# Layer 1 attention: float32r scores accumulated by key differences, two heads a pass, masking by zero values

## The chip, the core and the metric

One Trainium2 chip, one core. The core has five engines: TensorE (PE in the profile; its weight loads are PEld), VectorE (DVE), ScalarE (ACT), GpSimd (POOL) and SyncE (SP), which here only issues DMA transfers. Sixteen DMA engines move data between HBM and the on-chip memory SBUF. Matrix products land in PSUM, eight banks of 128 partitions by 512 fp32 values. The metric is the device time of one execution in microseconds (us), taken as the median of several runs; a profile is one further execution, recorded by the hardware.

## What is computed

Sixteen batches of x (512 rows of 256) and a context (1601 rows of 256) with an integer mask go through two layers, each an attention and a feed-forward part. Only the attention of layer 1 is changed:

```
xn = layernorm(x)
q, k, v = xn @ Wq.T + bq, ctx @ Wk.T + bk, ctx @ Wv.T + bv     # 16 heads of 16
scores  = q k^T / sqrt(16);  scores = where(mask == 0, -1e9, scores)
x = x + softmax(scores) v @ Wo.T + bo
```

Layer 0 is a local attention (a window of 64 keys) and a recurrent gate over the batches; the last part of layer 1 is a mixture of 8 experts of which each token takes 2.

## The kernel before

The kernel has three stages, one after the other. Layer 0 (to about 1366 us of the span) also prepares, late in the stage, the keys of batch 0 for layer 1. The attention of layer 1 follows (its scores run from 1440 to 4796 us), and then the experts (from 4875 us). Inside each stage the program order is written out by hand: `at(when, fn, ...)` puts a piece of work at a chunk number, the pieces are sorted by it, and every engine and the DMA queue of SP take their instructions in that order. The queue of SP is served in order: an instruction that waits holds back all that follow it.

**Loops of layer 1.** A batch has 16 heads in `NG` = 4 groups of 4, and its 1601 keys (padded to `SKP` = 1604) in `NCH` = 13 chunks of 128, the last of 65. The main loop (line 1318) counts chunks `n`; a batch takes `PER` = 52 of them, all batches 832. In each chunk it issues:

- `score` (line 1205): for each of the four heads, the transposed scores of one key chunk (128 keys by 512 queries) as an fp32 product with 32 rows of contraction, into one of four PSUM banks "e"; then four exponentials on ACT into `pt`. The 32 rows of a head are 16 of the head's components, one row that adds the mask bias, one that adds the negative row maximum, and 14 unused ones. The operands `ke` and `qe` are loaded by `load_ke` and `load_qe`.
- `value` (line 1222) for the chunk before: probabilities times values, four heads side by side in one PSUM bank "pv". Each head's values have a seventeenth column of ones, which sums the probabilities. With three pairs of maxima in a chunk it comes in two halves of 256 queries.
- `max_pair` (line 961), two or three times: row maxima for a group that comes 18 chunks later (`LEAD`). Here queries and keys are split in a high and a low half of their bits (`split`, line 154), stacked to 64 rows for a head (16 components times four combinations of high and low), and multiplied as float32r, two heads at a time, into two of three PSUM banks "m"; DVE reduces each bank.
- whatever `at` has put at this chunk: projections, normalisation, loads, stores, routing.

**Keys.** `key_pieces` (line 150) makes the keys of a batch: `project`, `mean`, `fill`, `add`; then `halve` stores them to `ke_d` and splits them, and `store` writes the halves to `ks_d`, each half twice (`r` is the place among the four combinations). All of this goes through HBM: `ks_d` is read back by `load_ks` (one transfer of 128 partitions for a pair of heads, 802 KB), `ke_d` by `load_ke` (one of 802 KB for a group).

**Maxima.** `shift_a` and `shift_b` (lines 984 and 991) reduce the maxima, turn them and store them into the row of `qe_d` that the scores read. **Mask.** `apply_masks` (line 368) makes bias rows, `mask_bias` (line 912) copies them into `ke_d`; `constant_rows` (line 334) fills the fixed rows of both tensors during layer 0.

Of the kernel before, what the change touches and what calls it, by code (L numbers as in the profile page):

```python
# [21 lines left out]
P = 128  # L22
# [36 lines left out]
def tile_kernel(ctx: ExitStack, tc: tile.TileContext, a, out):  # L59
# [73 lines left out]
    ke_d = [dram.tile([NG, P, SKP], F32, name=f"ke_d{i}") for i in range(2)]  # L133
    qe_d = [dram.tile([NG, P, S], F32, name=f"qe_d{i}") for i in range(2)]
    ks_d = [dram.tile([H // 2, P, SKP], F32, name=f"ks_d{i}") for i in range(2)]
    qs_d = [dram.tile([H // 2, P, S], F32, name=f"qs_d{i}") for i in range(2)]
    m_d = dram.tile([B, SKP], F32, name="m_d")
    mb_d = dram.tile([B, SKP], F32, name="mb_d")
# [5 lines left out]
    def stacked(t_d, m, r):  # L144
        return t_d[4 * m : 4 * m + 4].rearrange("p (h r d) n -> (p h) r d n", h=2, r=4)[:, r]

    def slotted(t_d, m):
        return t_d[2 * m : 2 * m + 2].rearrange("g (j s) n -> (g j) s n", s=32)[:, 0:HD, :]

    def key_pieces(pool, bank, bufs, pieces=2):  # L150
# [23 lines left out]
        def project(b, m, i):  # L174
# [3 lines left out]
            if i == 0:  # L178
                st[b, m, "k"] = pool.tile([P, SKP], F32, name="kc", bufs=bufs.get("kc", 2))
                st[b, m, "sum"] = pool.tile([P, 4], F32, name="ksum")  # L180
            ps = bank()
            for k in range(2):
# [8 lines left out]
                out=st[b, m, "k"][:, c0 : c0 + n],  # L191
# [17 lines left out]
        def part_of(h):  # L209
            return slice(h * KN, (h + 1) * KN)  # L210
# [8 lines left out]
        def add(b, m, h):  # L219
            k = st[b, m, "k"][:, part_of(h)]  # L220
            nc.vector.scalar_tensor_tensor(
                k, k, cols[:, BK1 + m : BK1 + m + 1], st.pop((b, m, "u")), ALU.add, ALU.add
            )

        def halve(b, m, h):
            k = st[b, m, "k"][:, part_of(h)]
            nc.sync.dma_start(out=slotted(ke_d[b % 2], m)[:, :, part_of(h)], in_=k)
            st[b, m, h, "halves"] = split(k, "k", KN)

        def store(b, m, h):  # L230
            hi, lo = st.pop((b, m, h, "halves"))
            for r, t in ((0, hi), (2, hi), (1, lo), (3, lo)):
                nc.sync.dma_start(out=stacked(ks_d[b % 2], m, r)[:, :, part_of(h)], in_=t)

# [9 lines left out]
            store=store,  # L244
        )


    with ExitStack() as l0:
# [80 lines left out]
        krow = wp.tile([P, SKP // 4], F32)  # L329
        nc.gpsimd.tensor_copy(krow, cols[:, KROW : KROW + 1].to_broadcast([P, SKP // 4]))  # L330
        qrow = wp.tile([P, S // 4], F32)
        nc.gpsimd.tensor_copy(qrow, cols[:, QROW : QROW + 1].to_broadcast([P, S // 4]))

        def constant_rows(i, g):
            for t_d, row in ((ke_d, krow), (qe_d, qrow)):
                nc.sync.dma_start(
                    out=t_d[i][g].rearrange("p (r n) -> p r n", r=4),
                    in_=row[:, None, :].to_broadcast([P, 4, row.shape[-1]]),
                )

# [3 lines left out]
        def load_masks():  # L346
            n = n4
            mask_i = wp.tile([n, SKP // 4], I32)
            nc.sync.dma_start(out=mask_i, in_=a["mask"].rearrange("b (r n) -> (b r) n", r=4))
            mask["i"] = mask_i  # L350

        def count_masks():
# [13 lines left out]
            mask.update(keep=keep, count=count, own=own, dg=dg)  # L366

        def apply_masks():
            n, keep, count, own, dg = (n4, *(mask[i] for i in ("keep", "count", "own", "dg")))
# [5 lines left out]
            nc.vector.tensor_mul(dg, own, qscale[0:n, :])  # L375
            nc.vector.tensor_reduce(count, dg, AX.X, ALU.add)
            nc.vector.tensor_single_scalar(count, count, 1.0e9 * HD**0.5, op=ALU.mult)
            nc.vector.tensor_scalar(keep, keep, 1.0, count, ALU.subtract, ALU.mult)
            nc.sync.dma_start(out=mb_d.rearrange("b (r n) -> (b r) n", r=4), in_=keep)
# [364 lines left out]
        for i in range(2 * NG):  # L744
            at(58 + 16 * i, constant_rows, i // NG, i % NG)
# [3 lines left out]
        for m in range(2):  # L749
# [5 lines left out]
            for h in range(4):  # L755
                at(o + 64 + 16 * h, keys.fill, 0, m, h)
                at(o + 69.5 + 16 * h, keys.add, 0, m, h)
                at(o + 73.5 + 16 * h, keys.halve, 0, m, h)
                at(o + 77 + 16 * h, keys.store, 0, m, h)
# [24 lines left out]
    with ExitStack() as l1:  # L784
# [23 lines left out]
        for t in vts:  # L808
            nc.gpsimd.memset(t, 0.0)
            nc.gpsimd.memset(  # L810
                t[:, :, 0 : H * VW].rearrange("p c (h d) -> p c h d", d=VW)[:, :, :, HD : HD + 1],
                1.0,
            )
# [3 lines left out]
        LEAD = 18  # L817

# [68 lines left out]
        def project_q(b, m):  # L887
# [14 lines left out]
            state[b]["qc", m] = qc, *keys.split(qc, "q", S)  # L902

        def store_q(b, m):
            qc, hi, lo = state[b].pop(("qc", m))
            nc.sync.dma_start(out=slotted(qe_d[b % 2], m), in_=qc)
            for r, t in ((0, hi), (1, hi), (2, lo), (3, lo)):
                nc.sync.dma_start(out=stacked(qs_d[b % 2], m, r), in_=t)

        keys = key_pieces(pool, bank, {})  # L910

        def mask_bias(b):
            rows_d = ke_d[b % 2].rearrange("g (j s) n -> (g j) s n", s=32)
            nc.sync.dma_start(
                out=rows_d[:, HD, :], in_=mb_d[b : b + 1, :].to_broadcast([H, SKP])
            )
# [8 lines left out]
        def project_v(b, p):  # L925
# [3 lines left out]
            for c in range(2 * p, min(2 * p + 2, NCH)):  # L929
                kn, o = kn_of(c), (c - 2 * p) * P  # L930
                for k in range(2):
# [8 lines left out]
            nc.scalar.copy(  # L940
                vts[p][0:kn, 0:n, 0 : H * VW].rearrange("p c (h d) -> p c h d", d=VW)[
                    :, :, :, 0:HD
                ],
                ps[0:kn, 0 : n * D].rearrange("p (c h d) -> p c h d", c=n, h=H),
# [5 lines left out]
        def load_ks(b, p):  # L950
            kst[b, p] = pool.tile([P, SKP], F32R, name="ks", bufs=3)
            nc.sync.dma_start(out=kst[b, p].bitcast(F32), in_=ks_d[b % 2][p])

        def load_qs(b, g):
            qst[b, g] = pool.tile([P, 2, S], F32R, name="qs")
# [35 lines left out]
        def shift_b(b, g):  # L991
# [4 lines left out]
            nc.vector.tensor_copy(nmT, ps[0:HD, 0:P])  # L996
            nc.sync.dma_start(
                out=qe_d[b % 2][g, HD + 1 : P : 32, :].rearrange("j (q p) -> j q p", p=P),
                in_=nmT,
            )  # L1000

        kts, qts = {}, {}

        def load_ke(b, g):
            kts[b, g] = pool.tile([P, SKP], F32, name="ke")
            nc.sync.dma_start(out=kts[b, g], in_=ke_d[b % 2][g])

        def load_qe(b, g):
            qts[b, g] = pool.tile([P, S], F32, name="qe")
            nc.sync.dma_start(out=qts[b, g], in_=qe_d[b % 2][g])  # L1010
# [191 lines left out]
        probs = {}  # L1202
        pvs = {}

        def score(b, g, c):
            kt, qt, kn = kts[b, g], qts[b, g], kn_of(c)
            scs = [psum.tile([P, S], F32, name="e", tag="e", bufs=4) for j in range(4)]
            for j, sc in enumerate(scs):
                r0 = 32 * j
                nc.tensor.matmul(  # L1210
                    sc[0:kn, :],
                    lhsT=kt[r0 : r0 + 32, c * P : c * P + kn],
                    rhs=qt[r0 : r0 + 32, :],
                    start=True,
                    stop=True,
                )
            for j, sc in enumerate(scs):
                pt = pool.tile([P, S], F32, name="pt", bufs=NPT)
                nc.scalar.activation(pt[0:kn, :], sc[0:kn, :], AF.Exp)  # L1219
                probs[b, g, c, j] = pt  # L1220
# [25 lines left out]
        for b in range(B):  # L1246
            s0 = b * PER
            at(s0 - 58, mask_bias, b)
            if b:
                at(s0 - 81, keys.mask_rows, b)  # L1250
            for m, os, o in (
                (0, (-75, -73, -71, -68), (-67, -67, -64, -62, -60, -63, -60, -58, -56)),
# [337 lines left out]
```

## Time and profile before

| | us |
|---|---|
| median of 3 runs | 5832.95 (5831.14 to 5835.01) |
| the profiled execution, its own time | 5856.85 |
| its span, first to last instruction | 5855.0 |
| layer 0, to the first product of the maxima | 1366.6 |
| layer 1, first to last score | 3355.9 |
| experts, first product to the end | 980 |

Over the span PE is busy for 5518.5 us (94%), DVE for 3405.4 (58%), ACT for 2629.4 (45%) and POOL for 1699.5 (29%). The DMA engines moved 806 MB, 138 GB/s in the mean. The largest groups of instructions, in busy us:

| line, engine | what | count | busy, mean of one |
|---|---|---|---|
| L980 DVE | reduction of a bank of maxima | 4096 | 2125.1, 569 ns |
| L1219 ACT | exponential of a score bank | 3328 | 1716.6, 601 ns |
| L972 PE | product for the maxima, float32r | 4096 | 1031.8, 453 ns |
| L1210 PE | score product, fp32 | 6656 | 982.7, 645 ns |
| L1232 PE | value product, fp32 | 9656 | 977.0, 476 ns |

Products that occupy different rows or columns of the array run at the same time, so a group's busy time is less than count times mean. An fp32 product appears as two records. A line such as `L972 PE MATMUL m<-ks,qs 64*128 64x400 f32 x2` reads: line 972, engine PE, written tile m from tiles ks and qs, 64 rows of contraction by 128 columns of weights, 400 columns streamed, two records; before it stand the start and the time until the last record's end, in us. A transfer in the DMA view counts packets, of which the small ones close a transfer.

### The profile page before, as it was taken

What the parts mean: (1) busy time and instruction counts of PE and PEld (TensorE: products, weight loads), DVE (VectorE), ACT (ScalarE), POOL (GpSimd) and SP (SyncE); (2) the same over time, 40 slices, a digit from 0 to 9 for tenths busy, and PEclk for the clock granted to TensorE, in tenths of its full rate; (3) what the DMA queues carried; (4) which work ended last, traced back from release to release, by engine and by line L of the source; (5) the groups of instructions that cost most, each with busy time, mean ns of one, the idle gap of its engine ahead of it and who ended that gap; (6) DMA issues with size and microseconds to landing.
All of it is one profiled execution on the core that took longest, in us unless ns stands there. A gap on an engine that the chain in (4) does not pass through costs nothing. (4 is left out here: it accounts for less than half of the span.)

```text
span 5855.0 us, 95951 instructions
## 1 busy us (share of the span) xinstructions
PE 5518.5 (94%) x36550; PEld 2706.0 (46%) x36550; DVE 3405.4 (58%) x9214; ACT 2629.4 (45%) x5250; POOL 1699.5 (29%) x1328
## 2 busy tenths in 40 slices
PE   7888888887999999999999999999999987999999
PEld 4555445444334334334334334334333335776776
DVE  5555555525777777777777777777777731111111
ACT  3444444421555555555555555555555551222221
POOL 3555555422122222222212213212222012222222
PEclk7999999886999999999999999999999998999999
DMA  4444444424445455444554544544544312222211
GB/s 155 154 150 145 132 134 134 137 74 159 141 151 187 159 169 174 164 166 164 173 173 159 181 157 153 199 143 163 191 159 164 122 50 78 72 77 71 65 63 46
DMA packets 356255, 806.46 MB, mean 138 GB/s; under 512 B 47566, under 2 KB 139202, under 8 KB 353619
## 3 DMA queue, kind: packets, MB, share of 16 engines
q1 hardware_dynamic: 336594, 752.25, 38.4%
q0 software_dynamic: 19200, 48.08, 2.4%
q8 instruction: 288, 4.72, 0.3%
q14 instruction: 173, 1.41, 0.1%
HBM read 479.60 MB, written 326.73 MB: 138 GB/s over the span
## 5 line engine op out<-in xcount | busy, mean ns | idle before, releaser
L980 DVE TENSOR_REDUCE pm<-m 128x1 f32<-128x402 f32 (+1 forms) x4096 | 2125.1, 569 | 629.8 <-PE m L972 609.2
L1219 ACT ACTIVATE pt<-e 128x512 f32<-128x512 f32 (+1 forms) x3328 | 1716.6, 601 | 1182.3 <-PE e L1210 1182.3
L972 PEld LDWEIGHTS m<-ks,qs 64*128 64x128 f32 x4096 | 465.9, 186 | 1371.2 <-DVE pm L980 879.3
L972 PE MATMUL m<-ks,qs 64*128 64x402 f32 (+1 forms) x4096 | 1031.8, 453 | 16.9 <-DVE pm L980 14.1
L1210 PE MATMUL e<-qe,ke 32*128 32x512 f32 x6656 | 982.7, 645 | 0.0
L1232 PE MATMUL pv<-pt,vt 128*32 128x256 f32 (+2 forms) x9656 | 977.0, 476 | 0.0
L1417 ACT ACTIVATE hT<-h,cols 128x384 f32<-128x384 f32 (+1 forms) x320 | 199.5, 624 | 753.6 <-PE h L1409 753.6
L1437 PE MATMUL y<-w,hT 128*128 128x256 f32 x2176 | 476.3, 379 | 0.0
L1409 PE MATMUL h<-xeT,w 128*128 128x384 f32 (+1 forms) x1280 | 475.8, 530 | 0.0
L1437 PEld LDWEIGHTS y<-w,hT 128*128 128x128 f32 x2176 | 410.4, 190 | 54.4
L512 DVE CUSTOM_DVE_ANT_0 tmp<-s,cst 128x192 f32<-128x192 f32 (+1 forms) x1024 | 279.2, 336 | 222.1 <-PE s L500 221.1
L1210 PEld LDWEIGHTS e<-qe,ke 32*128 32x128 f32 x6656 | 272.7, 180 | 262.9 <-issue 220.4
L563 DVE TENSOR_TENSOR pt<-s,cst 128x384 f32<-128x384 f32 (+2 forms) x768 | 248.0, 391 | 201.8 <-PE s L548 197.4
L564 ACT ACTIVATE pt<-pt 128x384 f32<-128x384 f32 (+2 forms) x768 | 242.8, 389 | 230.7 <-DVE pt L563 230.7
L1409 PEld LDWEIGHTS h<-xeT,w 128*128 128x128 f32 x1280 | 243.8, 191 | 213.7 <-issue 115.2
L1449 POOL DMA_INDIRECT out<-y_t,xe x136 | 134.8, 991 | 588.7 <-DVE y_t L1446 583.9
L1232 PEld LDWEIGHTS pv<-pt,vt 128*32 128x32 f32 (+1 forms) x9656 | 191.2, 108 | 247.4 <-issue 245.4
L1394 DVE COPY xeT<-tp 128x384 f32<-128x384 f32 (+1 forms) x80 | 45.2, 606 | 446.8 <-PE tp L1391 446.8
L1191 POOL DMA_INDIRECT slots<-row,put x128 | 133.2, 1041 | 573.6 <-issue 480.0
L107 POOL TENSOR_TENSOR rs<-mo,mhalf 128x4 f32<-128x4 f32 x64 | 66.4, 1038 | 707.7 <-DVE mo L105 707.7
L214 POOL TENSOR_SCALAR u<-keep,kmean 128x802 f32<-128x802 f32 (+1 forms) x68 | 193.1, 2839 | 268.9 <-DVE kmean L205 250.3
L1445 DVE TENSOR_TENSOR y_t<-y,b 128x256 f32<-128x256 f32 x136 | 57.7, 425 | 359.0 <-PE y L1437 359.0
(192 smaller groups left out, 5586.4 us busy)
## 6 DMA issues: line engine op xcount, KB each, us to landing
ks<-ks_d SPq DMA_DIRECT2D x128, 802.0 KB
ke<-ke_d SPq DMA_DIRECT2D x64, 802.0 KB
ks_d<-khi SPq DMA_DIRECT2D x120, 401.0 KB
ks_d<-klo SPq DMA_DIRECT2D x120, 401.0 KB
raw_d<-raw SPq DMA_DIRECT2D x128, 256.0 KB
qs<-qs_d SPq DMA_DIRECT2D x64, 512.0 KB
cv<-in_ctxT SPq DMA_DIRECT2D x96, 256.0 KB
ctxT<-in_ctxT SPq DMA_DIRECT2D x60, 402.0 KB
```

Source lines behind the costliest of these rows:

```text
L214: nc.gpsimd.tensor_scalar(u, st[b, "keep"][:, part_of(h)], 1.0, st[b, m, "mean"], ALU.subtract, ALU.mult)
L512: nc.vector.tensor_tensor_reduce(out=tmp[:, lo:], in0=sc[j][:, i, lo:BW], in1=band[:, lo:], scale=1.0, scalar=NEG, op0=ALU.add, op1=ALU.ma ...
L563: nc.vector.tensor_tensor(t, sc[j][:, i, 0:w], c, ALU.min)
L564: nc.scalar.activation(t, t, AF.Exp)
L972: nc.tensor.matmul(sc[:, 0:n], lhsT=qs[r0 : r0 + 64, jp, q * P : (q + 1) * P], rhs=ks[r0 : r0 + 64, k0 : k0 + n], start=True, stop=True,)
L980: nc.vector.tensor_reduce(pms[b, g][:, q, 2 * jp + jj, part : part + 1], sc[:, 0:n], AX.X, ALU.max)
L1210: nc.tensor.matmul(sc[0:kn, :], lhsT=kt[r0 : r0 + 32, c * P : c * P + kn], rhs=qt[r0 : r0 + 32, :], start=True, stop=True,)
L1219: nc.scalar.activation(pt[0:kn, :], sc[0:kn, :], AF.Exp)
L1232: nc.tensor.matmul(pv[32 * j : 32 * j + 32, part], lhsT=vts[c // 2][0:kn, c % 2, v0 : v0 + 32], rhs=probs[b, g, c, j][0:kn, part], start=f ...
L1409: nc.tensor.matmul(ps[:, 0:n], lhsT=weights[e][0][:, k, m * P : (m + 1) * P], rhs=xeT[:, k, 0:n], start=(k == 0), stop=(k == 1),)
L1417: nc.scalar.activation(hT[:, m, 0:n], ps[:, 0:n], AF.Gelu, bias=cols[:, at : at + 1])
L1437: nc.tensor.matmul(ps[:, 0:D], lhsT=hT[:, m, t * P : (t + 1) * P], rhs=weights[e][1][:, m, :], start=(m == 0), stop=(m == NH - 1),)
```

## The change

The scores of layer 1 are no longer an fp32 product over 32 rows. They use the float32r product over 64 rows that the maxima already use, with the same `qs` tiles, two heads at a time. To keep them accurate, each of the four score banks of a group is kept over all 13 chunks: it is first set to the negative row maximum by an fp32 product of ones with a tile `shift`, and each chunk then adds the product with the *difference* between its keys and those 128 places before (`differ`; the first chunk's difference is with zeros, for which the key tile has 128 zero columns in front). The differences are split, stored to `kd_d` and loaded by `load_kd` in five runs of two or three chunks. `score` comes in two halves of a chunk: heads 0 and 1 where all four were, heads 2 and 3 behind the first part of `value`.

Masked keys are handled by multiplying values, and the column of ones, by 0 or 1 (`kept`), in place of a bias on the scores. So `ke_d`, `qe_d`, `mb_d`, `constant_rows` and `mask_bias` go. `ks_d` and `kd_d` hold each half once (32 rows for a head), and the loads read every row twice, by a repeat of 2 in the source. The maxima reach `shift` by way of a small tensor `nm_d`.

```diff
@@ halves in HBM
-    ks_d = [dram.tile([H // 2, P, SKP], F32, name=f"ks_d{i}") for i in range(2)]
+    ks_d = [dram.tile([H // 2, 2, 2, HD, SKP], F32, name=f"ks_d{i}") for i in range(2)]
+    kd_d = [dram.tile([H // 2, 2, 2, HD, SKP], F32, name=f"kd_d{i}") for i in range(2)]
...
         def halve(b, m, h):
-            k = st[b, m, "k"][:, part_of(h)]
-            nc.sync.dma_start(out=slotted(ke_d[b % 2], m)[:, :, part_of(h)], in_=k)
-            st[b, m, h, "halves"] = split(k, "k", KN)
+            st[b, m, h, "halves"] = split(st[b, m, "k"][:, part_of(h, P)], "k", KN)
         def store(b, m, h):
-            hi, lo = st.pop((b, m, h, "halves"))
-            for r, t in ((0, hi), (2, hi), (1, lo), (3, lo)):
+            for r, t in enumerate(st.pop((b, m, h, "halves"))):
                 nc.sync.dma_start(out=stacked(ks_d[b % 2], m, r)[:, :, part_of(h)], in_=t)
+        def differ(b, m, h):
+            k = st[b, m, "k"]
+            u = pool.tile([P, KN], F32, name="u", bufs=1)
+            nc.gpsimd.tensor_sub(u, k[:, part_of(h, P)], k[:, part_of(h)])
+            st[b, m, "u"] = u
+        def halve_d(b, m, h):
+            st[b, m, h, "halves"] = split(st.pop((b, m, "u")), "k", KN)
+        def store_d(b, m, h):
+            for r, t in enumerate(st.pop((b, m, h, "halves"))):
+                nc.sync.dma_start(out=stacked(kd_d[b % 2], m, r)[:, :, part_of(h)], in_=t)
@@ values
-            nc.scalar.copy(vts[p][0:kn, 0:n, ...], ps[...])
+            for c in range(n):
+                nc.scalar.activation(
+                    vt[:, c, :, 0:HD],
+                    ps[0:kn, c * D : (c + 1) * D].rearrange("p (h d) -> p h d", h=H),
+                    AF.Copy,
+                    scale=keep[:, c : c + 1],
+                )
+            nc.gpsimd.tensor_copy(
+                vt[:, :, :, HD], keep[:, :, None].to_broadcast([kn, n, H])
+            )
@@ loads
         def load_ks(b, p):
             kst[b, p] = pool.tile([P, SKP], F32R, name="ks", bufs=3)
-            nc.sync.dma_start(out=kst[b, p].bitcast(F32), in_=ks_d[b % 2][p])
+            for h in range(2):
+                nc.sync.dma_start(
+                    out=kst[b, p].bitcast(F32)[64 * h : 64 * h + 64, :],
+                    in_=ks_d[b % 2][p, h]
+                    .rearrange("r d n -> (r d) n")[None]
+                    .to_broadcast([2, 2 * HD, SKP]),
+                )
...
+        runs = ((0, 3), (3, 6), (6, 9), (9, 11), (11, NCH))
+        def load_kd(b, g, i):
+            c0, c1 = runs[i]
+            n = min(c1 * P, SKP) - c0 * P
+            t = pool.tile([P, 2, 3 * P], F32R, name="kd", bufs=3)
+            for jp in range(2):
+                for h in range(2):
+                    nc.sync.dma_start(
+                        out=t.bitcast(F32)[64 * h : 64 * h + 64, jp, 0:n],
+                        in_=kd_d[b % 2][2 * g + jp, h, :, :, c0 * P : c0 * P + n]
+                        .rearrange("r d n -> (r d) n")[None]
+                        .to_broadcast([2, 2 * HD, n]),
+                    )
@@ shift_b
+            nc.sync.dma_start(out=nm_d[g % 2], in_=nmT)
             nc.sync.dma_start(
-                out=qe_d[b % 2][g, HD + 1 : P : 32, :].rearrange("j (q p) -> j q p", p=P),
-                in_=nmT,
-            )
+                out=shifts[g % 2][0:P:32, :], in_=nm_d[g % 2].rearrange("(j q) p -> j (q p)", j=4)
+            )
@@ score
-        def score(b, g, c):
+        def score(b, g, c, jp):
+            kn = kn_of(c)
+            if c == 0 and jp == 0:
+                banks[b, g] = [psum.tile([P, S], F32, name="e", tag="e", bufs=4) for j in range(4)]
+                for j, sc in enumerate(banks[b, g]):
+                    r0 = 32 * j
+                    nc.tensor.matmul(sc, lhsT=ones[r0 : r0 + 32, :],
+                        rhs=shifts[g % 2][r0 : r0 + 32, :], start=True, stop=True)
+            kd, o = kds[b, g, c]
+            scs = banks[b, g][2 * jp : 2 * jp + 2]
+            for jj, sc in enumerate(scs):
+                r0 = 64 * jj
                 nc.tensor.matmul(
                     sc[0:kn, :],
-                    lhsT=kt[r0 : r0 + 32, c * P : c * P + kn],
-                    rhs=qt[r0 : r0 + 32, :],
-                    start=True,
+                    lhsT=kd[r0 : r0 + 64, jp, o : o + kn],
+                    rhs=qst[b, g][r0 : r0 + 64, jp, :],
+                    start=False,
                     stop=True,
+                    skip_group_check=True,
                 )
@@ order
-            at(s0 - 58, mask_bias, b)
+                    at(s0 + od[3 * h], keys.differ, b, m, h)
+                    at(s0 + od[1 + 3 * h], keys.halve_d, b, m, h)
+                    at(s0 + od[2 + 3 * h], keys.store_d, b, m, h)
-                at(first + 7, load_ke, b, g)
-                at(last + 2, load_qe, b, g)
+                for i, (c, _) in enumerate(runs):
+                    at(s0 + g * NCH + c - 4, load_kd, b, g, i)
...
-                score(b, g, c)
+                score(b, g, c, 0)
...
                     value(n - 1, part)
+                if live and i == 0:
+                    score(b, g, c, 1)
```

In layer 0, batch 0's keys get the same three new pieces between the old ones, and the mask is also loaded by chunk (four small transfers) and turned by two transposes into `kept`. The tile `qs` has three buffers in place of two.

## Prediction

> **What bounds the kernel now.** I first split the span into its stages, because the change touches the second alone (layer 1, from the first score to the last; the columns are busy time with counts, granted clock, share of the sixteen DMA engines, GB/s).
>
> ```profile
> core 0: us, PE busy (x) PEld busy (x) DVE busy (x) ACT busy (x) POOL busy (x), PEclk, DMA share, GB/s
> 0.00:1366.60 1366.60, 1141.28 (x9704) 657.98 (x9704) 680.80 (x3258) 556.25 (x1317) 648.93 (x497) 0.89 0.42 135
> 1440.60:4796.50 3355.90, 3319.29 (x22913) 1311.33 (x22916) 2491.64 (x5444) 1865.71 (x3600) 738.52 (x528) 0.99 0.47 161
> 4875.00:5855.00 980.00, 969.92 (x3728) 685.84 (x3728) 168.91 (x352) 200.75 (x321) 273.66 (x272) 0.99 0.21 66
> ```
>
> In layer 1 PE is busy for 3319 of 3356 us at clock 0.99: it sets the pace; DVE has 74%, ACT 56%, POOL 22%, the DMA engines 47%. That is 64 groups of four heads (16 batches of 4), 52.4 us each, 13 key chunks to a group. The timeline of PE shows what a chunk is made of:
>
> ```profile
> 2704.11 1.14 PE L1210 MATMUL e<-qe,ke 32*128 32x512 f32 x8
> 2705.18 0.45 PE L972 MATMUL m<-ks,qs 64*128 64x400 f32 x2
> 2705.56 0.64 PE L1232 MATMUL pv<-pt,vt 128*32 128x256 f32 x8
> 2706.13 0.61 PE L972 MATMUL m<-ks,qs 64*128 64x400 f32 x2
> 2706.66 0.64 PE L1232 MATMUL pv<-pt,vt 128*32 128x256 f32 x8
> 2707.23 0.46 PE L972 MATMUL m<-ks,qs 64*128 64x402 f32 x2
> 2707.63 1.14 PE L1210 MATMUL e<-qe,ke 32*128 32x512 f32 x8
> ```
>
> From start to start, four heads' fp32 scores hold PE for 1.07 us, a float32r pair of the maxima for 0.38 us.
>
> Then I asked how many of the sixteen DMA engines a transfer uses, since the change rewrites every key load. Three quiet stretches: the tail of a ke load (rows of 6416 B, 128 partitions outermost), a raw store (rows of 2048 B, 128 outermost), and two rb loads (2048 B, whose source has eight heads outermost and then a repeat of 16).
>
> ```profile
> 4729.00:4729.50 0.50, 0.50 (x5) 0.00 (x0) 0.26 (x1) 0.25 (x1) 0.00 (x0) 1.00 1.01 423
> 4767.75:4768.05 0.30, 0.30 (x8) 0.00 (x0) 0.00 (x0) 0.30 (x2) 0.15 (x1) 1.00 0.98 382
> 4812.10:4815.10 3.00, 0.00 (x0) 0.00 (x0) 0.00 (x0) 0.00 (x0) 0.37 (x1) 0.50 0.51 159
> ```
>
> The share is about 1 for the first two and 0.51 for rb: eight engines work and eight stand idle. The DMA view of one stretch each (a shift row load of four rows, a raw store, the two rb loads) says the same by counting the packets under 512 B, which close a transfer, one on each engine it used:
>
> ```profile
> DMA packets 8, 0.01 MB, mean 23 GB/s; under 512 B 4, under 2 KB 4, under 8 KB 8
> ...
> DMA packets 144, 0.26 MB, mean 291 GB/s; under 512 B 16, under 2 KB 16, under 8 KB 144
> ...
> DMA packets 272, 0.52 MB, mean 138 GB/s; under 512 B 16, under 2 KB 16, under 8 KB 272
> ```
>
> Four rows outermost: 4 engines. 128: 16. Eight outermost: 16 for two transfers, 8 each. The outermost count of the source decides.
>
> **The decisive edit: the key loads.** load_ks and load_kd copy each row twice by a repeat of 2 that stands outermost in the source ([2, 32, n] into 64 partitions). By the rows above such a transfer gets two engines. No row here has a 2, so I bound it by the rule. The Trainium skill (DMA: Bandwidth & Descriptors, Rules for kernel authors) says that the slowest dimension that isn't 1 sets how many engines share a transfer, and that a leading zero-stride broadcast of c copies confines it to at most c. The rows alone (16, 8, 4, always the outermost count) leave open whether a zero-stride level counts, since rb's repeat stands inside. If it doesn't count, the 32 rows behind it give 16 engines and the loads stay hidden; by the rule all of them queue on the same two. I go with the rule, and size it from rows of the trace.
>
> Per group, each of the two engines then moves:
> - ks: two pairs, two transfers each, 32 rows of 6416 B for each engine: 128 x 6416 = 821 KB. One engine's rate is 423/(1.01 x 16) = 26.2 GB/s: 31.3 us.
> - kd: 2 pairs x 2 heads x 5 runs, the same 821 KB in rows of 1536, 1024 and 784 B. Nearest rows are those of 2048 B: 382/(0.98 x 16) = 24.4 GB/s in raw, 159/(0.51 x 16) = 19.5 in rb: 33.7 to 42.1 us. I take 37.
> - everything else. In a steady batch (next view) the engines are busy 0.49 x 218.7 / 4.01 groups = 26.7 us each per group. ks, ke and qe (2.7 MB on sixteen) are 6.5 of it, which leaves 20.2. The transfers with eight outermost (ks_d, ke_d, qs_d, qe_d, comp, rb: 2.97 MB per group) weigh 15.5 us on eight engines, 7.7 in the mean; so 12.5 + 15.5 = 28 on those eight, less 2.8 for ke_d and qe_d, is 25. These durations include crowding among sixteen (all rows of 2048 B: 99 ns in the mean, 84 when quiet), so 21 to 25; I take 22. ks_d and kd_d together store what ks_d alone stored.
> - idle between: shift_b's row goes out to nm_d, and the queue of SP waits for its landing before it issues the next loads, once a group: 2 to 4 us, taken 3.
>
> ```profile
> 2501.90:2720.60 218.70, 211.47 (x1456) 84.34 (x1455) 160.74 (x353) 117.16 (x226) 50.45 (x37) 0.98 0.49 165
> ...
> ks<-ks_d SPq DMA_DIRECT2D x8, 802.0 KB
> ke<-ke_d SPq DMA_DIRECT2D x4, 802.0 KB
> ks_d<-khi SPq DMA_DIRECT2D x8, 401.0 KB
> ks_d<-klo SPq DMA_DIRECT2D x8, 401.0 KB
> ```
>
> Sum: 31.3 + 37 + 22 + 3 = 93.3 us per group, against 52.4 now and about 45 of compute. The loads run at most four or five chunks ahead (kd has three buffers and is issued at c - 4), but the two engines always hold the next ks or kd, so compute waits and they do not. Layer 1 becomes 64 x 93.3 = 5971 us, +2615. On the profiled execution that is 5856.9 + 2615 = 8472; the median of the runs stands 24 lower, so **8450**.
>
> **The other edits**, which lie beside those waits; without that cover they cost or gain what is said.
> - Scores. 1.07 us per chunk goes. Two float32r pairs of 512 columns come, in the same 64-row form as the maxima beside them. Above: each a slot of its own, 0.38 + 112 columns, about 0.43. Below: they share the change of form; 256 more fp32 columns cost the value product 0.42 us of its 0.99, so 0.15 is fixed there, and a pair without that is about 0.29; the maxima lose theirs too. Gain 0.2 to 0.6 us, taken 0.5: 832 x 0.5 = 416 us. The shift product comes, 64 x 1.07 = 68. Net 348 us on PE, worth nothing while PE waits for kd.
> - DVE: halve_d, 60 x 0.57 (as khi) = 34 us. POOL: differ and its lo, 120 x 1.95 (as klo) = 234; the column of keep in vt, 112 x about 1; the kc memsets less. POOL has 738 of 3356. ACT: 112 copies become 208 of 0.37 (the 65x256 form): +15.
> - SP: 20 kd and 2 more ks issues per group, less ke, qe, one store: about +19 x 0.33 to 0.6 = 6 to 12 us in 93. Queued behind a blocked SP are the next stores and loads of x, ctxT and cv; they lead by five chunks.
> - Layer 0: 16 constant-row pairs and the mb_d store go; mask by chunk, two transposes and batch 0's differences come (16 POOL and 8 DVE pieces): within 15 us either way. The last stage is untouched.
>
> **Rivals.**
> 1. The zero-stride level doesn't count, or the repeat is laid inside: sixteen engines. kd then adds some 2 us per engine to a share of 0.49, hidden, and PE sets the pace: 5833 - 348 = **5480** (5380 to 5730); DVE, 2526 of about 3000 us, would begin to hold it. It decides from about six engines up, where 68 x 2/6 + 22 = 45 us equals compute. For it: a source may repeat, and rb shows no penalty for its inner one. Against: the counts of 4, 8 and 16. 6%.
> 2. Transfers and compute take turns. PE's clock was 0.50 in the rb stretch, where it stood idle, so after each wait compute starts slowly, and the three kd buffers may leave the engines empty. If half of 45 us is uncovered: 93 + 22 = 115, so 5833 + 64 x 63 = **9870**. For it: SP waits in order, as its 620 us behind raw show. Against: 16 us of ks stand in the queue twice a group. 6%.
> 3. Sixteen engines, and no gain on PE (float32r at 512 columns no faster than fp32): +68, **5900**, or about the same where half is gained. The 0.38 us of 400 columns speaks against it. 2%.
>
> **How the numbers follow.** Two engines as the bound: 86%, 8450, own range 7750 (80 us per group would give 7600, 85 gives 7900) to 9500 (110 us). With half of rival 2 the range to 9600 holds 8 in 10; rival 1 stays outside. A measurement of this kernel tells about 0.2% from no change. Faster: rival 1, 0.06. Same: half of rival 3, 0.01. Slower: the rest, 0.93.
>
> **What would show it.** Right: a group lasts 85 to 110 us; PE's share in layer 1 falls to about half with the clock below 0.99; score L1210's successor waits for kd, a maximum for ks; a stretch of ks loads alone shows a DMA share near 0.13 at about 50 GB/s; the share over layer 1 falls below 0.47. Wrong: groups of 45 to 48 us, kd landing within its four chunks at a share near 1, and PE still at 95% or more.

## The result

The changed kernel takes 8617.15 us (median of four runs, 8605.12 to 8624.01) against 5833.98 us before: a ratio of 1.476, 95% interval 1.474 to 1.479. The profiled execution took 8624.01 us, with a span of 8622.2. Almost all of the loss lies where the prediction put it: from the first score to the last, layer 1 takes 6110.2 us in place of 3355.9, and the rest of the span 2512 in place of 2499.

The windows of the changed kernel (columns as in the prediction: busy time and counts of the five engines, granted clock, share of the sixteen DMA engines, GB/s): layer 1 as a whole, then a stretch in which only a ks pair was on its way, then one with kd rows alone.

```profile
1456.90:7567.10 6110.20, 3837.97 (x20103) 1629.09 (x20102) 2507.18 (x5503) 1970.11 (x3694) 977.17 (x782) 0.72 0.27 89
6231.00:6245.00 14.00, 9.56 (x64) 4.58 (x62) 7.75 (x17) 4.57 (x9) 0.00 (x0) 0.98 0.13 35
5098.00:5104.00 6.00, 5.96 (x44) 2.40 (x42) 4.68 (x11) 3.54 (x7) 3.48 (x4) 1.00 0.13 49
```

A group lasts 6110.2 / 64 = 95.5 us (before 52.4). No engine is near full: PE has 63% of layer 1 at clock 0.72, DVE 41%, and the sixteen DMA engines together 27%. The last two rows say why a low share is no sign of spare room: 0.13 is 2/16. The packet counts of the same two stretches (ks first) agree:

```profile
DMA packets 79, 0.49 MB, mean 35 GB/s; under 512 B 2, under 2 KB 2, under 8 KB 79
...
DMA packets 196, 0.29 MB, mean 49 GB/s; under 512 B 6, under 2 KB 196, under 8 KB 196
```

A kd transfer is 64 rows; 190 row packets are three of them (short of two rows at the window's edges), with six closing packets, two for each. So each of these loads ran on two engines. Counted from the start and duration of every packet in the trace, exactly two were on their way in 57% of the time over the steady groups (groups 12 to 51); before the change, in 1% of layer 1. Exactly four were on their way in under 2%, although ks and kd loads stand in the queue together: that speaks for the same two engines in all of them.

The page shows what that does to the engines. Its heading, two of its forty-slice rows, and the four groups that answer to the table of before (busy us and mean ns of one; then the engine's idle time before them and what ended most of it):

```profile
span 8622.2 us, 94680 instructions
...
PE   7888886666666566666665656656566666679999
...
PEclk8999986777777777777677767777767676789999
...
L1017 DVE TENSOR_REDUCE pm<-m 128x1 f32<-128x402 f32 (+1 forms) x4096 | 2111.3, 569 | 3295.7 <-PE m L1009 1871.5
L1279 ACT ACTIVATE pt<-e 128x512 f32<-128x512 f32 (+1 forms) x3328 | 1816.0, 597 | 3842.6 <-PE e L1269 3802.8
L1009 PE MATMUL m<-ks,qs 64*128 64x402 f32 (+1 forms) x4096 | 1327.8, 467 | 1214.1 <-DMA qs<-qs_d 910.5
L1269 PE MATMUL e<-qs,kd 64*128 64x512 f32 (+1 forms) x3328 | 1122.2, 558 | 1074.9 <-DMA kd<-kd_d 1073.3
```

DVE and ACT wait for PE, and PE waits for two DMA loads: the score product 1073.3 us for kd, the product for the maxima 910.5 us for qs. The edit never touched the qs load, but it stands behind the key loads in SP's queue. (Experiments 2 and 3 below show behind which: with ks on sixteen engines this wait falls to 162 us, with kd on sixteen it stays at 830.) The view of waits gives the same with count and longest wait, in which 1073.3 us are 334 waits of up to 15.7 us:

```profile
PEld e L1269 <- DMA kd<-kd_d: 1203.3, 375, 16.5
PE e L1269 <- DMA kd<-kd_d: 1073.3, 334, 15.7
PE m L1009 <- DMA qs<-qs_d: 910.5, 47, 23.3
```

In a stretch where PE waits for nothing, its timeline (start, time to the last record's end) shows the gain that the edit does bring:

```profile
5101.94 0.50 PE L1269 MATMUL e<-qs,kd 64*128 64x512 f32 x2
5102.28 0.35 PE L1009 MATMUL m<-ks,qs 64*128 64x400 f32 x2
5102.56 0.64 PE L1292 MATMUL pv<-pt,vt 128*32 128x256 f32 x8
5103.13 0.50 PE L1269 MATMUL e<-qs,kd 64*128 64x512 f32 x2
```

A score pair and a maxima pair together hold PE for 5102.56 - 5101.94 = 0.62 us. A chunk with two maxima pairs needs 2 x 0.62 = 1.24 us where it needed 1.07 + 2 x 0.38 = 1.83: 0.59 us less (both figures from one chunk each).

### The profile page after: what moved, and what is told of

It is laid out like the page before. It is cut to its first block, busy times and chain, and to the rows that moved or that the text cites. A ratio compares the mean times of both kernels' runs of the same rounds, so it can differ in the third digit from the quotient of the medians.

```text
span 8622.2 us, 94680 instructions
## 1 busy us (share of the span) xinstructions
PE 6026.6 (70%) x33736; PEld 3019.8 (35%) x33736; DVE 3430.8 (40%) x9285; ACT 2733.0 (32%) x5346; POOL 1960.6 (23%) x1600
## 5 line engine op out<-in xcount | busy, mean ns | idle before, releaser
L1279 ACT ACTIVATE pt<-e 128x512 f32<-128x512 f32 (+1 forms) x3328 | 1816.0, 597 | 3842.6 <-PE e L1269 3802.8
L1009 PE MATMUL m<-ks,qs 64*128 64x402 f32 (+1 forms) x4096 | 1327.8, 467 | 1214.1 <-DMA qs<-qs_d 910.5
L1269 PE MATMUL e<-qs,kd 64*128 64x512 f32 (+1 forms) x3328 | 1122.2, 558 | 1074.9 <-DMA kd<-kd_d 1073.3
L1009 PEld LDWEIGHTS m<-ks,qs 64*128 64x128 f32 x4096 | 670.4, 229 | 1676.5 <-issue 1251.5
L1292 PE MATMUL pv<-pt,vt 128*32 128x256 f32 (+2 forms) x9656 | 1240.3, 586 | 0.0
L1269 PEld LDWEIGHTS e<-qs,kd 64*128 64x128 f32 (+1 forms) x3328 | 440.8, 215 | 2133.9 <-DMA kd<-kd_d 1203.3
L158 POOL TENSOR_TENSOR klo<-u,khi 128x802 f32<-128x802 f32 (+1 forms) x68 | 124.7, 1833 | 1499.6 <-DVE khi L155 1256.2
L1093 POOL TENSOR_TENSOR comp<-comp,rb 128x512 f32<-128x512 f32 x32 | 40.6, 1269 | 987.2 <-DMA rb<-rec_d 925.5
L956 PE MATMUL m<-wv,cv 128*128 128x256 f32 (+1 forms) x832 | 261.2, 466 | 0.9 <-DMA cv<-in_ctxT 0.9
L181 PE MATMUL m<-ctxT,wk_w 128*128 128x402 f32 (+1 forms) x480 | 245.7, 644 | 15.0 <-DMA ctxT<-in_ctxT 15.0
```

What stands on the lines that cost most here:

```text
L181: nc.tensor.matmul(ps[:, 0:n], lhsT=wk1[:, k, m * P : (m + 1) * P], rhs=ck[:, k, 0:n], start=(k == 0), stop=(k == 1),)
L956: nc.tensor.matmul(ps[0:kn, 2 * o : 2 * o + D], lhsT=cv[:, k, o : o + kn], rhs=wv1[:, k, :], start=(k == 0), stop=(k == 1),)
L1009: nc.tensor.matmul(sc[:, 0:n], lhsT=qs[r0 : r0 + 64, jp, q * P : (q + 1) * P], rhs=ks[r0 : r0 + 64, k0 : k0 + n], start=True, stop=True,)
L1269: nc.tensor.matmul(sc[0:kn, :], lhsT=kd[r0 : r0 + 64, jp, o : o + kn], rhs=qst[b, g][r0 : r0 + 64, jp, :], start=False, stop=True, skip_gr ...
L1292: nc.tensor.matmul(pv[32 * j : 32 * j + 32, part], lhsT=vts[c // 2][0:kn, c % 2, v0 : v0 + 32], rhs=probs[b, g, c, j][0:kn, part], start=f ...
```

## The experiments

Two theories stood to be told apart first. **Two engines**: the repeat that stands outermost in the source confines each load to two engines, and those two are the bound. **The rest of the change**: more and smaller transfers through one queue (24 key loads for a group where there were 3), or the new order of scores and exponentials, would make it slow on sixteen engines too. Group times below are the layer 1 window over 64; ratios are against the kernel before on the same chip.

**1. The repeat inside.** Same transfers, same bytes, same rows; in the source the 32 rows now stand ahead of the repeat, so partitions 2i and 2i+1 hold the same row, and the queries are stored to match.

```diff
-                    .rearrange("r d n -> (r d) n")[None]
-                    .to_broadcast([2, 2 * HD, SKP]),
+                    .rearrange("r d n -> (r d) n")[:, None]
+                    .to_broadcast([2 * HD, 2, SKP]),
...
-                        .to_broadcast([2, 2 * HD, n]),
+                        .to_broadcast([2 * HD, 2, n]),
... (store_q)
-            rows_d = qs_d[b % 2][4 * m : 4 * m + 4].rearrange("p (h r d) n -> (p h) r d n", h=2, r=4)
-            for r, t in enumerate(state[b].pop(("qc", m))):
-                for i in range(2):
-                    nc.sync.dma_start(out=rows_d[:, 2 * r + i], in_=t)
+            rows_d = qs_d[b % 2][4 * m : 4 * m + 4].rearrange(
+                "p (h r d c) n -> (p h) r c d n", h=2, r=2, c=2
+            )
+            for c, t in enumerate(state[b].pop(("qc", m))):
+                for r in range(2):
+                    nc.sync.dma_start(out=rows_d[:, r, c], in_=t)
```

> The repeat of 2 is laid behind the 32 rows in the sources of ks and kd ([32, 2, n] in place of [2, 32, n]), and the query halves are stored in the matching row order; the number of transfers, their bytes and everything else stay. Two-engine theory: the outermost count is 32, so sixteen engines share each load; ks and kd together take 8.5 us of an engine per group where they took 69 on two. PE sets the pace again: 45 to 48 us per group, 5480 us (5380 to 5730), PE busy over 95% of layer 1, DMA share about 0.5. Rival 'transfers by their number' (24 loads per group issued in order by SP): unchanged, 8600. Rival 'compute chain' (scores in halves, banks held over 13 chunks, PE at a lower clock): unchanged, 8600.

Measured: 5781.51 us, ratio 0.990 (0.987 to 0.993), 51.3 us a group. Its layer 1:

```profile
1430.00:4710.80 3280.80, 3112.07 (x20103) 1387.12 (x20104) 2486.30 (x5503) 1927.87 (x3694) 982.93 (x782) 0.97 0.60 166
```

The DMA share rises from 0.27 to 0.60, PE's clock from 0.72 to 0.97, and the score product's wait for kd falls from 1073 us to 47.5. The order of two dimensions in the source is worth a third of the kernel's time. What the second theory names is all still there, and the kernel is no slower than before (1.0% faster). But it lies above the range expected, 302 us over the 5480 of rival 1. PE's own pace may be lower still: with the 0.59 us of the timeline above it would be 5834 - (832 x 0.59 - 68) = 5411, an estimate. Experiments 4 and 6 to 8 look for the difference.

**2 and 3. One of the two loads on sixteen engines.** Each transfer with the repeat becomes two plain ones of 32 rows; in experiment 2 for kd alone, in experiment 3 for ks alone.

```diff
... (experiment 2, load_kd)
-                    nc.sync.dma_start(
-                        out=t.bitcast(F32)[64 * h : 64 * h + 64, jp, 0:n],
-                        in_=kd_d[b % 2][2 * g + jp, h, :, :, c0 * P : c0 * P + n]
-                        .rearrange("r d n -> (r d) n")[None]
-                        .to_broadcast([2, 2 * HD, n]),
-                    )
+                    for i in range(2):
+                        r0 = 64 * h + 32 * i
+                        nc.sync.dma_start(
+                            out=t.bitcast(F32)[r0 : r0 + 32, jp, 0:n],
+                            in_=kd_d[b % 2][2 * g + jp, h, :, :, c0 * P : c0 * P + n].rearrange(
+                                "r d n -> (r d) n"
+                            ),
+                        )
... (experiment 3, load_ks)
-                    .rearrange("r d n -> (r d) n")[None]
-                    .to_broadcast([2, 2 * HD, SKP]),
+                for i in range(2):
+                    r0 = 64 * h + 32 * i
+                    nc.sync.dma_start(
+                        out=kst[b, p].bitcast(F32)[r0 : r0 + 32, :],
+                        in_=ks_d[b % 2][p, h].rearrange("r d n -> (r d) n"),
+                    )
```

> Only the kd loads change: each transfer with the repeat becomes two plain ones of 32 rows (40 per group in place of 20), the same bytes; ks stays with the repeat outermost. Two-engine theory: the two engines lose 37 of their 95 us per group and gain 2.3 from sixteen-engine rows: ks 31.6 + the rest 25 + 2.3 + idle 3 = 62 us per group, 8617 - 64 x 33.5 = 6470 us (6250 to 6700). Transfers by their number: 20 more per group at about half a us each, slower than 8617, near 9250. Compute chain: unchanged, 8600.

> Only the ks loads change: each transfer with the repeat becomes two plain ones of 32 rows (8 per group in place of 4); kd stays with the repeat outermost. Two-engine theory: kd 37.4 + the rest 25 + 2 + idle 3 = 67.5 us per group, 8617 - 64 x 28 = 6825 us (6600 to 7100). Transfers by their number: 4 more per group, 8650 to 8750. Compute chain: unchanged, 8600.

Measured: experiment 3, 6788.1 us, ratio 1.162 (1.158 to 1.166), 67.0 us a group; experiment 2, 7766.53 us, ratio 1.329 (1.325 to 1.334), 82.0 us. The windows, 3 and then 2:

```profile
1436.30:5723.60 4287.30, 3559.74 (x20103) 1540.46 (x20102) 2501.94 (x5503) 1955.27 (x3694) 977.37 (x782) 0.83 0.43 127
```

```profile
1450.70:6701.20 5250.50, 3586.50 (x20103) 1557.96 (x20104) 2507.15 (x5503) 1943.96 (x3694) 979.33 (x782) 0.77 0.36 104
```

With ks freed, the sum of the two engines' remaining work holds to half a microsecond (67.5 expected). With kd freed (62 expected), it fails by far: ks alone is less time on the pair (31.3 us against 37 in the prediction's sum), and yet the group is 15 us longer. In experiment 2 the two engines seem not to be full (the trace doesn't say on which engine a packet ran): exactly two packets were on their way in only 36% of the time (29.5 of 82 us, about what ks needs), none at all in 10%, against 4% in the changed kernel. A new wait stands in SP's queue:

```profile
SPq L1050 <- DMA ks<-ks_d: 2169.0, 250, 11.8
```

These are 250 waits of 8.7 us, for 256 ks transfers, each at the issue of a kd load; the changed kernel has no such wait. Why an issue waits there (the kd tile doesn't depend on ks) no run here settles; experiment 2 has 40 kd transfers a group, and its timeline shows one run's eight of them standing behind the ks pair:

```profile
3021.58 1.08 SPq L984 DMA_DIRECT2D ks<-ks_d  x2
3022.77 20.37 SPq L1050 DMA_DIRECT2D kd<-kd_d  x8
3043.24 0.63 SPq L241 DMA_DIRECT2D kd_d<-khi  x1
3043.97 0.62 SPq L241 DMA_DIRECT2D kd_d<-klo  x1
3044.68 7.31 SPq L1050 DMA_DIRECT2D kd<-kd_d  x8
```

The eight behind the pair take 20.37 us, the next eight 7.31. So a new theory, still to be tested: **a ks pair on two engines is a burst of some 16 to 20 us, longer than the lead of the loads behind it** (four chunks, 14 us if a group's 13 chunks take 45 us of compute), and whatever stands behind it in the queue comes late.

**4. One transfer for each pair.** Experiment 1 with half as many key loads, 12 a group.

```diff
-            for h in range(2):
-                nc.sync.dma_start(
-                    out=kst[b, p].bitcast(F32)[64 * h : 64 * h + 64, :],
-                    in_=ks_d[b % 2][p, h]
-                    .rearrange("r d n -> (r d) n")[:, None]
-                    .to_broadcast([2 * HD, 2, SKP]),
-                )
+            nc.sync.dma_start(
+                out=kst[b, p].bitcast(F32),
+                in_=ks_d[b % 2][p]
+                .rearrange("h r d n -> (h r d) n")[:, None]
+                .to_broadcast([4 * HD, 2, SKP]),
+            )
... (load_kd likewise)
```

> As e1, and both heads of a pair come in one transfer (64 rows outermost, the repeat inside): 12 loads of ks and kd per group in place of 24. Two-engine theory: the loads are hidden in e1 already, so the time is that of e1 within 0.5%. Transfers by their number, as a second limit behind the first: some 380 us under e1 (12 x 0.5 us x 64).

Measured: 5704.67 us, ratio 0.977 (0.974 to 0.979), 50.3 us a group, 77 us less than experiment 1. Halving the number of key loads gains something, but far from the 380 us that their number was given in the expectation, and it isn't what keeps the kernel from 5480. What the 77 us come from isn't shown: a ks row of 6416 B also takes 245 ns in the median here, and 439 in experiment 1. Its layer 1, and from the groups of a steady stretch of 2050 us the reduction of the maxima and their weight load:

```profile
1427.90:4645.50 3217.60, 3085.94 (x20103) 1369.23 (x20104) 2487.36 (x5503) 1929.34 (x3694) 981.06 (x782) 0.97 0.53 169
```

```profile
L1018 DVE TENSOR_REDUCE pm<-m 128x1 f32<-128x402 f32 (+1 forms) x2560 | 1312.8, 568 | 330.8 <-PE m L1010 309.3
...
L1010 PEld LDWEIGHTS m<-ks,qs 64*128 64x128 f32 x2560 | 350.9, 189 | 301.5 <-DVE pm L1018 218.0 <-issue 71.9 <-DVE ksum L188 4.4
```

DVE is busy for 77% of layer 1, and yet some weight loads of the maxima wait for a bank that it hasn't read (218 us of this stretch).

**5. Each kd half stored twice, loads of 128 plain rows.** On the changed kernel: kd on sixteen engines as in experiment 2, but with 10 kd loads a group in place of 40. If many transfers through the queue were what failed in experiment 2, this would mend it.

```diff
-    kd_d = [dram.tile([H // 2, 2, 2, HD, SKP], F32, name=f"kd_d{i}") for i in range(2)]
+    kd_d = [dram.tile([H // 2, 2, 4, HD, SKP], F32, name=f"kd_d{i}") for i in range(2)]
... (store_d writes each half twice; load_kd, once for each jp)
-                        in_=kd_d[b % 2][2 * g + jp, h, :, :, c0 * P : c0 * P + n]
-                        .rearrange("r d n -> (r d) n")[None]
-                        .to_broadcast([2, 2 * HD, n]),
+                    in_=kd_d[b % 2][2 * g + jp, :, :, :, c0 * P : c0 * P + n].rearrange(
+                        "h r d n -> (h r d) n"
+                    ),
```

> Against the changed kernel: each half of the differences is stored twice (64 rows for a head), so that kd loads are one plain transfer of 128 rows for a pair (10 per group in place of 20, sixteen engines); ks keeps its repeat outermost. Theory 'two engines, and in the run with plain kd halves the SP queue stood behind ks landings because 40 small loads came after them': with 10 loads the sum holds, ks 31.6 + the rest 27 + 2 + idle 3 = 63 us per group, 6540 us (6250 to 6850). Theory 'ks on two engines costs about 80 us per group whatever the kd loads do': near that run, 7600 to 7800.

Measured: 7413.84 us, ratio 1.270 (1.266 to 1.274), 76.6 us a group: between the two ranges expected, far nearer to the one in which a confined ks costs about 80 us whatever kd does. The wait of kd issues for ks landings has gone from 2169 to 83 us, so that wait is not what makes a ks pair expensive. Its layer 1 and the waits that are left:

```profile
1450.40:6355.90 4905.50, 3478.45 (x20103) 1500.17 (x20104) 2499.46 (x5503) 1940.86 (x3694) 977.85 (x782) 0.79 0.40 121
```

```profile
PEld e L1271 <- DMA kd<-kd_d: 777.4, 100, 15.9
PE e L1271 <- DMA kd<-kd_d: 755.8, 78, 15.0
PE m L1012 <- DMA qs<-qs_d: 511.5, 39, 19.5
```

The product still waits for kd, on sixteen engines now, in few and long waits of up to 15.9 us. The ks transfers, the only key loads still confined, are not what the view names: PE waits for what stands behind them. A part of the longer group is PE itself, which works more slowly between waits: it is busy for 3478 us in layer 1 at a granted clock of 0.79, against 3086 at 0.97 in experiment 4, for the same products. That is 6 of the 26 us by which a group is longer.

**6, 7, 8. What holds the sixteen-engine version.** All on experiment 4. Experiment 6 issues the scores of heads 2 and 3 right behind those of heads 0 and 1; experiment 7 reduces half of the columns of each bank of maxima (it leaves out the maximum over the other half); experiment 8 does both.

```diff
... (6 and 8, main loop)
                 score(b, g, c, 0)
+                score(b, g, c, 1)
...
-                if live and i == 0:
-                    score(b, g, c, 1)
... (7 and 8, max_pair)
-                    pms[b, g][:, q, 2 * jp + jj, part : part + 1], sc[:, 0:n], AX.X, ALU.max
+                    pms[b, g][:, q, 2 * jp + jj, part : part + 1], sc[:, 0 : n // 2], AX.X, ALU.max
```

> On the merged loads: the scores of heads 2 and 3 come right behind those of heads 0 and 1, ahead of the maxima and the value product. Chain theory (the value product waits for the exponentials of heads 2 and 3, which start only when the second half of the scores is done): most of the 210 us of PE gain that the merged kernel does not show comes back, 5500 to 5600 us against 5705. VectorE theory (its reductions, 77% of layer 1 and in bursts, hold the maxima's banks): 5705 within 30 us, or slower by up to 60, since the maxima come later in the chunk.

> On the merged loads: each reduction of the maxima reads only the first half of its columns (leaves out the maximum over the other half of the keys); products and everything else stay. VectorE theory: 5480 us or less, since 4096 reductions shrink from 0.57 to about 0.36 us. Chain theory: 5705 within 40 us.

> Scores together and half reductions at once (leaves out the maximum over half of the keys). If each theory holds a part: under both single runs, near PE's own sum of 45 us per group, 5380 to 5450 us. If only one counts: equal to the better of the two within 30 us.

| | us | ratio (95%) | us a group | against experiment 4 |
|---|---|---|---|---|
| 6 | 5643.84 | 0.966 (0.964 to 0.969) | 49.6 | -61 |
| 7 | 5540.67 | 0.949 (0.946 to 0.952) | 48.0 | -164 |
| 8 | 5463.74 | 0.936 (0.933 to 0.939) | 46.6 | -241 |

Experiments 6 and 7 each lie between the figures of the two theories, and 8 lies 14 us above its range: each theory holds a part. The two gains add, nearly (61 + 164 = 225, measured 241). Layer 1 of experiment 8, and the reduction in experiment 7:

```profile
1422.60:4407.50 2984.90, 2877.00 (x20097) 1339.19 (x20100) 1731.61 (x5503) 1862.57 (x3694) 987.80 (x782) 0.98 0.57 182
```

```profile
L1018 DVE TENSOR_REDUCE pm<-m 128x1 f32<-128x201 f32 (+1 forms) x4096 | 1303.5, 361 | 1050.3 <-PE m L1010 1044.4
```

With 361 ns for a reduction in place of 568, and the scores together, PE is busy for 96% of layer 1 and the kernel stands at 5464, a ratio of 0.936. So PE's gain is real. Of the 241 us between experiments 4 and 8, DVE holds the larger part (busy for 77% and in bursts), the order of scores and exponentials the smaller. That 5464 is so near to the 5480 of rival 1 is partly chance, since rival 1 took 0.5 us a chunk where 0.59 was read off. Experiment 6 does all of the work and is, with experiment 10, the best version here: 3.4% faster than the kernel before.

**9 and 10. The loads earlier.** To test the burst: kd in runs of two chunks with five buffers, issued seven chunks ahead, and ks four and three chunks earlier. Experiment 9 puts that on experiment 5, experiment 10 on experiment 6, where no load is late and nothing should change.

```diff
-        runs = ((0, 3), (3, 6), (6, 9), (9, 11), (11, NCH))
+        runs = tuple((c, min(c + 2, NCH)) for c in range(0, NCH, 2))
-            t = pool.tile([P, 2, 3 * P], F32R, name="kd", bufs=3)
+            t = pool.tile([P, 2, 2 * P], F32R, name="kd", bufs=5)
-                at(first - 5, load_ks, b, 2 * g)
-                at(first, load_ks, b, 2 * g + 1)
+                at(first - 9, load_ks, b, 2 * g)
+                at(first - 3, load_ks, b, 2 * g + 1)
-                    at(s0 + g * NCH + c - 4, load_kd, b, g, i)
+                    at(s0 + g * NCH + c - 7, load_kd, b, g, i)
```

> Against the run with kd stored twice (ks on two engines, kd plain, 76.6 us per group): kd in runs of two chunks with five buffers, issued 7 chunks ahead in place of 4, and ks issued four chunks (first of a group) and three chunks (second) earlier; bytes and engines per transfer stay. Burst theory (the 16 us that a ks pair holds two engines delays the kd and qs transfers issued behind it, twice a group, beyond their lead of four chunks): with the longer lead the wait is covered, and what is left is compute of about 50 us or the two engines' sum of 63: 6540 to 6860 us. Theory 'ks on two engines costs its full 31.6 us per group in any order': 7300 to 7500.

> The same earlier loads on the version with sixteen-engine merged loads and the scores together. If its loads are hidden, as the two theories of its limit (VectorE's reductions, the exponentials) say: 5644 us within 0.5%. If late loads are part of its limit (its first group of a batch takes 54 us where others take 49): 5580 to 5610.

Measured: experiment 10, 5643.66 us, ratio 0.966 (0.964 to 0.967), as experiment 6; experiment 9, 7146.8 us, ratio 1.222 (1.220 to 1.225), 72.1 us a group: 267 us less than experiment 5, and between what was expected of the one theory and of the other. In experiment 9 PE hardly waits for kd any more (32 us, at most 0.8 at a time) and not for qs, but for loads that it had hardly waited for before:

```profile
PE m L959 <- DMA cv<-in_ctxT: 458.4, 32, 18.9
PE m L181 <- DMA ctxT<-in_ctxT: 402.9, 48, 15.6
```

In experiment 5 there is no such wait for cv, and 21.5 us for ctxT. SP itself also stands longer before the second transfer of `shift_b` (142.0 us in experiment 5):

```profile
SPq L1038 <- DMA nm_d<-nmT: 561.2, 64, 13.3
```

So kd's wait can be bought off with an earlier issue, and the delay then shows at other transfers of the same queue. That a ks pair on two engines holds up what stands behind it is supported by experiments 2, 5 and 9; how the 72 us divide among those transfers stays open.

The starts of the shift products show more. In the steady groups of experiment 9 the four groups of a batch take 89.8, 49.9, 75.4 and 82.4 us, and three, one, two and two ks pairs are issued in them. With one pair a group runs at experiment 4's pace, so a ks pair need not cost its 16 us; but that group has the least other traffic too, and no run here separates the two.

## Why the prediction was right

It said 8450 us, and 8617 was measured, 2.0% more and inside the likeliest case's own range. Its steps:

- **Two engines for a load with the repeat outermost.** Shown: six closing packets for three loads, a share of 0.13, and experiment 1, where the same bytes in the same number of transfers run in 5782. The rule that the prediction weighed against the rows for rb (the Trainium skill, DMA: Bandwidth & Descriptors, Rules for kernel authors) is borne out in its case: a zero-stride level of two counts when it leads, and when it stands inside, as in experiment 1, it doesn't confine.
- **The sum of a group**, in us on each of the two engines; measured in the steady groups (12 to 52, which last 97.9):

| | predicted | measured | how |
|---|---|---|---|
| ks | 31.3 | 31.6 to 36.1 | 128 rows of 247 ns (median) to 282 (mean) |
| kd | 37 | 38 | 1536, 1024 and 784 B packets: 52.9, 12 to 14, 10.1 engine-us, over two |
| nothing on its way | 3 | 3.7 | 3.8% of 97.9 |
| everything else | 22 | 20 to 25 | what is left |
| sum | 93.3 | 97.9 (95.5 over layer 1) | |

  The mis-sized term is ks: 245 ns for a row had been taken from the quiet tail of a ke load on all sixteen engines, and the mean on the loaded pair was 282. (Such rows already had a mean of 282 over layer 1 before the change.) That makes 4.8 us, about the 4.6 by which a steady group is longer than the sum; kd and the rest differ by less than their own ranges. "Everything else" is only what is left over, so the table by itself can't show that the terms add; experiment 3 does. The total came nearer than the steady groups did: 4.6 us in each of 64 groups would make layer 1 294 us longer than predicted, and it was 139 longer. The groups of the first and the last batch are shorter (the last four take 91, 84, 60 and some 40 us), which the prediction didn't count on; so much of the agreement within 2.0% is luck.
- **"The two engines always hold the next ks or kd, so compute waits and they do not."** It held for the change as made, and experiment 3 gave the sum again (67.0). As a general reason it fails: experiments 2, 5 and 9 have only ks, of the key loads, on the pair, and a group still takes 72 to 82 us where the sum gave 62 or 63. Experiment 2 is longer than experiment 4 by 31.7 us, as much as the 31.6 of ks, but that agreement proves nothing: 7.8 of the 31.7 are PE busy for longer at the lower clock, and experiments 5 and 9 are longer by 26.4 and 21.8. So taking turns, rival 2's mechanism with its slower PE, is seen where ks alone is confined. In the change itself it cost little, with nothing on its way in 3.8% of the time; that kd loads kept the pair full is the likely reason, not a tested one.
- **PE's gain of 0.5 us a chunk, worth nothing here.** Right on both counts: 0.59 in a chunk that doesn't wait, and a kernel that is slower all the same.
- **What would show it.** Group 85 to 110: 95.5. Clock below 0.99: 0.72. DMA share below 0.47: 0.27. A score waits for kd: yes. PE's share "about half": 63%. "About 50 GB/s" for ks alone: 35 in that stretch, 49 for kd. "A maximum for ks": wrong, it waits for qs, which stands behind the key loads in the queue.
- **SP's issues at 0.33 to 0.6 us.** Wrong: 3.0 us for a kd load (last section), 59 us of a group where 6 to 12 had been added for all the new issues. It did no harm to the number, as long as the two engines are the bound.
- **Rival 1's 5480** as the price of sixteen engines was too low: 5782 with the repeat inside, 5705 with merged loads. Its remark that DVE "would begin to hold it" was a missing term: 164 us by experiment 7; the other is the order of scores, 61 by experiment 6. Whether about six engines would be the turning point wasn't tried.

## What to carry to other kernels

When a load repeats rows, put the rows, not the repeat, outermost in the source, and then count the closing packets of one transfer in the trace: they tell how many engines it really had, while a low mean DMA share can hide two full ones. If a slow transfer must stay, adding up engine time gives only a floor: compare the length of its burst with the lead of everything behind it in the same queue, tensors that the edit doesn't touch among them. And before a faster TensorE is paid for, look at how busy the engine that drains its banks is: at 77% and in bursts, DVE took back 164 us (experiment 7), more than a third of the 423 that PE's gain was worth by estimate (832 x 0.59, less 68 for the shift product).

## What was not expected of the hardware

Issuing a transfer isn't free when its engines are behind. SP's timeline in the changed kernel:

```profile
4020.68 4.25 SPq L984 DMA_DIRECT2D ks<-ks_d  x2
4024.97 19.92 SPq L1048 DMA_DIRECT2D kd<-kd_d  x4
...
4049.50 7.83 SPq L1048 DMA_DIRECT2D kd<-kd_d  x4
```

Four kd issues behind a ks pair occupy SP for 19.92 us, four others for 7.83. Over the kernel one kd issue takes 3.0 us in the mean, 59 us of each group; in experiment 1 the same 1280 issues take 0.76. All of SP's issues together take 5242 of the 6110 us of layer 1, and 1815 of 3281 in experiment 1. The prediction had counted 0.33 to 0.6 us for each. So two slow engines also hold back the transfers that would run on the other fourteen, by way of the queue that issues them. Why an issue takes longer when its engines are behind, no trace here shows.
